# Key and value sums of two tiles: three more sums in one PSUM accumulator, with ScalarE copies between, and 44 weighings on VectorE

## The chip, the cores and the metric

One core of a Trainium2 chip runs the whole kernel. The time is device microseconds of one execution; the number compared is the median of several runs. The engines are TensorE (PE, with its weight loads as PEld), VectorE (DVE), ScalarE (ACT), GpSimd (POOL) and SyncE (SP, which here only issues transfers). Each works through its own queue in order, and they meet through semaphores.

## The reference

A graph attention layer with a residual and a layer norm, all in 32-bit floats: 16 graphs ("batches") of 1024 nodes with 512 features, 8 heads of 64, and one sparse adjacency matrix shared by all batches. The biases are zero in the inputs.

```python
q = (x @ Wq + bq).reshape(b, n, H, HD)
k = (x @ Wk + bk).reshape(b, n, H, HD)
v = (x @ Wv + bv).reshape(b, n, H, HD)
scores = jnp.einsum('bqhd,bkhd->bhqk', q, k) / jnp.sqrt(jnp.float32(HD))
scores = scores + (1.0 - adj)[None, None, :, :] * -1000000000.0
attn = jax.nn.softmax(scores, axis=-1)
out = jnp.einsum('bhqk,bkhd->bqhd', attn, v).reshape(b, n, d)
y = out @ Wo + bo
return layernorm(x + y)          # over the features
```

## The kernel before

The kernel uses that the adjacency matrix has few ones. It sorts the nodes by degree, cuts them into eight tiles of 128, and then works on "blocks": a block is 128 queries with one key each. For a block, GpSimd gathers 128 rows of keys and values (tile kvg) from DRAM; VectorE multiplies query and key (qk, L1313) and sums over each head (s, L1317); ScalarE takes the exponential (L1328); the value row is then weighed with it. The weighing has two forms in `weigh`: eight ScalarE instructions, one for each head (L1341), or one VectorE instruction (L1345). `by_act` says which block takes which. VectorE adds the weighed values up (L1357), or, for the nodes of high degree, TensorE does with a 0/1 matrix (L1366, L1367). A finished tile is normalised, transposed (poT, oT), multiplied by Wo (po, L799), and ends in the residual, the norm and a scatter to the output.

Ahead of that, for each batch, x is gathered, transposed on TensorE (pxT, xT) and multiplied by the weights. Tiles go in pairs, four pairs (j = 0 to 3) to a batch. `pair` makes the list of TensorE units of one pair. The queries are plain products (pq: `q0` for the first tile of the pair, `q1` for the second; each is four units of the function `product`). Tile 1, whose nodes have a single key each, has no queries after batch 0, so in the first pair of a batch `q1` is empty; and in the batches from 2 on tile 0 has queries only in every second batch, so there `q0` can be empty too.

Keys and values of a pair are made with seven half-size products instead of eight, by a scheme of the Strassen-Winograd kind. The weights are combined once into T1 to T4, beside the quarters B11, B21 and B22. For each pair VectorE forms four combinations s1 to s4 of the transposed inputs (`combine`, L783 to L786). A unit is two matmuls of 128x512 in the source, four in the profile (32-bit operands pass in two). Before the change, the units write to an accumulator x (twice), an accumulator z (twice), and to three banks p6, p7, p4 taken from four shared "fill" banks, which also serve all other products. The sums between them are made outside TensorE:

- ScalarE copies x to e after the first unit (L969), and x to the key of tile 0 after the second (L835);
- VectorE makes w = p6 + e (L972), g = p7 + w (L975), the key of tile 1 as p4 + g (L979), the value of tile 1 as z + g (L984) after z's first unit, and the value of tile 0 as z + w (L988) after its second.

The very first pair of all is computed plainly; 63 pairs use the scheme.

The order of all instructions is written out by hand in a loop of steps, one for each block (the `while` loop near the end). A step issues the block work first, then the functions that were planned for it with `later` (copies out of PSUM among them), then TensorE units out of the list `fronts` (or those of a finished tile, `finishing`, which go first) as long as a credit lasts. A step's credit is a share of the batch's remaining work, weighted by `load_of`. A unit has a cost, a function and a condition. If the unit at the head of the list is not ready, nothing more of the list is issued in that step. A unit that needs a copy made earlier (x's and z's second) is ready once that copy has been issued to its engine.

Of the kernel before, what the change touches and what calls it, by code (L numbers as in the profile page):

```python
# [71 lines left out]
LAST_SHARE = 3.4  # L72
BIAS = 0.22

P = 128
# [103 lines left out]
def kernel(  # L179
# [75 lines left out]
    with ExitStack() as main:  # L255
# [480 lines left out]

        BOTH = {}
        X, XT, SX, KV, VSUM, NRM, Y, OT, PS = {}, {}, {}, {}, {}, {}, {}, {}, {}
        set_up = {}
# [12 lines left out]
        def transpose_x(b, t):  # L752
            def pe():
# [25 lines left out]

                def combine():  # L780
                    s = [work.tile([P, HD2], F32, tag=f"s{i}", name=f"s{i}_{b}_{t}", bufs=1 + i // 4) for i in (1, 2, 3, 4)]
                    x0, x1 = XT[b, t - 1], XT[b, t]
                    nc.vector.tensor_tensor(s[0], x1[:, 0:HD2], x1[:, HD2:D], op=OP.add)  # L783
                    nc.vector.tensor_tensor(s[2], x0[:, 0:HD2], x1[:, 0:HD2], op=OP.subtract)
                    nc.vector.tensor_tensor(s[1], s[0], x0[:, 0:HD2], op=OP.subtract)
                    nc.vector.tensor_tensor(s[3], x0[:, HD2:D], s[1], op=OP.subtract)  # L786
                    SX[b, t // 2] = s
# [4 lines left out]

        def product(name, lhs, w, out):

# [8 lines left out]

            return [(PRODUCT, lambda c=c: unit(c), None) for c in range(NPAIR)]

# [10 lines left out]
        def pair(b, j):  # L816
# [62 lines left out]
            def lone_product():  # L879
# [24 lines left out]

                return [(4 * BIAS, pe, None)]

            def lhs(i):
                return lambda c: XT[b, tt[i]][:, ts(c, P)]

            q0, q1 = (  # L910
                product(f"pq_{b}_{tt[i]}", lhs(i), W["q"], lambda p, i=i: out_q(i, p)) if b == 0 or tt[i] != ONE_KEY else []
                for i in range(2)
            )
            if j == 0 and b >= PAIRED_FROM:
                q0 = []
                if merged(b):
                    q0 = product(f"pq_{b}_0", lambda c: BOTH[b // 2][:, 1, c, :], W["q"], lambda p: out_q(0, p))
                    q0 += lone_product()
# [28 lines left out]

            def unit(bank, left, right, first, after, need):
                def pe():
                    if first:  # L950
                        R[bank] = fill_psum(f"p{bank}_{b}_{j}") if bank[0] == "p" else psum.tile(
                            [P, HALF], F32, tag=bank, name=f"{bank}_{b}_{j}", bufs=1
                        )
                    l = left()
                    for c in range(2):
                        nc.tensor.matmul(  # L956
# [4 lines left out]

                return [(2 * PRODUCT, pe, lambda: (need is None or need in R) and (b, j) in SX and bool(combined))]

            def temp(name):
                R[name] = work.tile([P, D], F32, tag=name, name=f"{name}_{b}_{j}", bufs=1)
                return R[name]

            def out_e():
                nc.scalar.copy(temp("e"), R["x"])  # L969

            def out_w():
                nc.vector.tensor_tensor(temp("w"), R["p6"], R["e"], op=OP.add)  # L972

            def out_g():
                nc.vector.tensor_tensor(temp("g"), R["p7"], R["w"], op=OP.add)  # L975

            def out_k1():
                kv = KV[b, tt[1]]
                nc.vector.tensor_tensor(kv[:, 0:D], R["p4"], R["g"], op=OP.add)  # L979
                send(1)  # L980
                later_last(1, lambda: norm(b, tt[1], kv[:, 0:D]))

            def out_v1():
                nc.vector.tensor_tensor(new_kv(1)[:, D:], R["z"], R["g"], op=OP.add)  # L984
                R["v1"] = True

            def out_v0():
                nc.vector.tensor_tensor(KV[b, tt[0]][:, D:], R["z"], R["w"], op=OP.add)  # L988
                send(0)

            def s(i):
                return lambda: SX[b, j][i - 1]

            units = []
            units += unit("x", lambda: a(0, 0), B11, True, out_e, None)
# [334 lines left out]
        def by_act(n):  # L1330
# [168 lines left out]
        def paced(share, n):  # L1499
# [16 lines left out]
        with tc.manual_schedule():  # L1516
# [21 lines left out]
            while n < total or plan or rest or urgent or done or finishing or spilled or lone_tiles or not guarded:  # L1538
# [53 lines left out]
                while credit > 0 or urgent:  # L1592
# [10 lines left out]
                    if not units:  # L1603
# [54 lines left out]
```

## Time and profile before

| | |
|---|---|
| median of 3 runs | 1856.82 us (1855.36 to 1866.84) |
| span of the profiled execution | 1840.4 us |
| own time of the profiled execution | only its span is given; the median of the runs is 16.4 us above it |
| PE busy | 1798.2 us, 98%, 5140 matmuls |
| VectorE busy | 1693.7 us, 92% |
| ScalarE busy | 1563.2 us, 85% |
| GpSimd busy | 1215.3 us, 66% |
| granted TensorE clock | 0.996 on average |

A row of the groups names line, engine, operation, the tiles written and read, the shape and the count; after the first bar the busy time in us and the mean ns of one, after the second the idle time just before and what ended it. A row of the waits reads "engine line <- what released it: total us, times, longest us". A row of the timeline reads start in us, length in us, engine and instruction; in brackets the idle time before it and what released it. Matmuls overlap one another, so their pace is read from start to start.

### The profile page before, as it was taken

The page shows a single profiled execution, that of the slowest core. Times are in us where ns is not written, and L with a number is a line of the kernel's source. Part 1 is how long each engine was busy: PE and PEld are TensorE (multiplying, and loading weights), DVE is VectorE, ACT ScalarE, POOL GpSimd, SP SyncE. Part 2 cuts the span into 40 slices and gives each one's busy share as a digit, 9 for nine tenths or more (in the row PEclk, how much of TensorE's full clock was granted, in tenths as well). Part 3 has the DMA queues.
Part 4 walks back from the last instruction along what each step waited for, and adds up shares of the span by engine and source line. Part 5 has one row for each costly group of instructions (what it writes and reads, how often), then busy time and mean ns, then how long its engine had stood idle before and what let it go on. Part 6 is the DMA issues. An engine that isn't in the chain of part 4 may idle for free.

```text
span 1840.4 us, 25352 instructions
## 1 busy us (share of the span) xinstructions
PE 1798.2 (98%) x5140; PEld 876.2 (48%) x5140; DVE 1693.7 (92%) x3473; ACT 1563.2 (85%) x6183; POOL 1215.3 (66%) x1142
## 2 busy tenths in 40 slices
PE   7999999999999999999999999999999999999997
PEld 3444454554444454444444445444544444444443
DVE  6889889999989999999999999999999999997986
ACT  3637869989889898999889988989799999987886
POOL 1367766766565776767757666677666767665786
PEclk9999999999999999999999999999999999999998
DMA  7358787989889899999988998999989999889995
GB/s 287 106 190 253 256 325 237 346 301 327 308 280 314 295 336 319 344 316 308 347 316 310 346 335 276 343 321 322 339 315 325 314 355 326 306 324 325 338 319 191
DMA packets 198791, 558.54 MB, mean 303 GB/s; under 512 B 33450, under 2 KB 33470, under 8 KB 198626
## 3 DMA queue, kind: packets, MB, share of 16 engines
q0 software_dynamic: 112640, 370.50, 59.3%
q1 hardware_dynamic: 82910, 180.52, 26.2%
q10 hardware_dynamic: 3076, 5.82, 0.9%
q14 instruction: 122, 1.00, 0.2%
q8 instruction: 43, 0.70, 0.2%
HBM read 420.30 MB, written 157.45 MB: 314 GB/s over the span
## 4 chain that ended last, share of the span: by engine, by line
PE 69%; DVE 10%; ACT 9%; DMA 4%; issue 3%; POOL 1%; SPq 0%; POOLq 0%; DVEq 0%; ACTq 0%
PE po L799 17%; PE pq L799 15%; PE pp L956 12%; PE z L956 9%; PE x L956 9%; ACT pv L1341 5%; DVE qk L1313 2%; PE poT L1401 2%; PE pxT L757 2%; PE sum L1367 2%; DVE s L1317 2%; PE sum L1366 2%; DVE pv L1357 1%; ACT sq_k L809 1%; DMA kvg<-kv_pair,place_row 1%
## 5 line engine op out<-in xcount | busy, mean ns | idle before, releaser
L1341 ACT ACTIVATE pv<-kvg,pv 128x64 f32<-128x64 f32 x3600 | 907.5, 341 | 0.0
L1292 POOL DMA_INDIRECT kvg<-kv_pair,place_row x462 | 526.7, 1140 | 307.4 <-ACT pv L1341 99.6
L799 PE MATMUL pq<-wq,xT 128*128 128x512 f32 x792 | 367.8, 596 | 0.0
L1317 DVE TENSOR_REDUCE s<-qk 128x8 f32<-128x512 f32 x530 | 360.7, 681 | 6.8
L799 PE MATMUL po<-wo,oT 128*128 128x512 f32 x792 | 359.3, 594 | 0.7 <-ACT oT L1405 0.7
L1313 DVE TENSOR_TENSOR qk<-qt,kvg 128x512 f32<-128x512 f32 x434 | 297.2, 685 | 1.1 <-DMA kvg<-kv_rows,key_row 0.6
L956 PE MATMUL x<-b,xT 128*128 128x512 f32 x504 | 237.3, 593 | 0.5 <-ACT e L969 0.4
L956 PE MATMUL pp<-t,s 128*128 128x512 f32 x504 | 237.0, 593 | 0.0
L1357 DVE TENSOR_TENSOR pv<-pv,pv 128x520 f32<-128x520 f32 x329 | 228.3, 694 | 4.3 <-ACT pv L1341 4.2
L799 PEld LDWEIGHTS po<-wo,oT 128*128 128x128 f32 x792 | 149.1, 191 | 170.0 <-issue 160.2
L799 PEld LDWEIGHTS pq<-wq,xT 128*128 128x128 f32 x792 | 148.4, 192 | 161.9 <-issue 149.9
L1010 POOL DMA_INDIRECT x<-in_x_dram,asked_row x120 | 133.0, 1108 | 77.8 <-issue 21.3
L1148 POOL DMA_INDIRECT out_dram<-y,asked_row x129 | 146.9, 1139 | 39.1 <-issue 21.2
L1328 ACT ACTIVATE pv<-s,absent 128x8 f32<-128x8 f32 x434 | 127.0, 294 | 44.0 <-DVE s L1317 40.8
L809 ACT ACTIVATE sq_k<-kv 128x128 bf16<-128x128 f32 x512 | 150.8, 301 | 6.4 <-DVE kv L979 3.4
L956 PEld LDWEIGHTS pp<-t,s 128*128 128x128 f32 x504 | 94.7, 191 | 108.1 <-issue 99.4
L956 PEld LDWEIGHTS x<-b,xT 128*128 128x128 f32 x504 | 94.2, 191 | 107.4 <-issue 99.0
L956 PE MATMUL z<-b,s 128*128 128x512 f32 x252 | 119.2, 596 | 7.0 <-DVE kv L984 7.0
L1246 POOL DMA_INDIRECT qg<-q_rows,query_row x96 | 104.4, 1088 | 28.4 <-issue 26.9
L956 PE MATMUL z<-t,s 128*128 128x512 f32 x252 | 118.6, 593 | 0.0
L956 PE MATMUL pp<-t,xT 128*128 128x512 f32 x252 | 118.5, 593 | 0.0
L1134 ACT ACTIVATE y<-y,stats 128x512 f32<-128x512 f32 (+1 forms) x128 | 102.7, 806 | 17.0 <-DVE stats L1129 17.0
(279 smaller groups left out, 2713.0 us busy)
## 6 DMA issues: line engine op xcount, KB each, us to landing
kv_pair<-kv SPq DMA_DIRECT2D x98, 512.0 KB
q_rows<-q SPq DMA_DIRECT2D x106, 256.0 KB
qt<-q_rows SPq DMA_DIRECT2D x98, 256.0 KB
residual<-x SPq DMA_DIRECT2D x83, 256.0 KB
y<-residual SPq DMA_DIRECT2D x83, 256.0 KB
kv_rows<-kv SPq DMA_DIRECT2D x15, 512.0 KB
kvg<-kv_pair,place_row POOLq DMA_INDIRECT x462, 6.9
kv_pair<-kv SPq DMA_DIRECT2D x28, 256.0 KB
```

What stands on the lines that cost most here:

```text
L799: nc.tensor.matmul(p, lhs(c), w[:, c, :], start=(c == 0), stop=(c == NPAIR - 1))
L809: nc.scalar.activation(sq, s[:, ts(h, P)], AF.Square, scale=scale, accum_out=sums[:, h:h + 1])
L956: nc.tensor.matmul(R[bank], l[:, ts(c, P)], right[:, c, :], start=(first and c == 0), stop=(c == 1), skip_group_check=True,)
L1010: nc.gpsimd.indirect_dma_start(out=y, out_offset=None, in_=x_rows, in_offset=bass.IndirectOffsetOnAxis(ap=asked_row[:, t:t + 1], axis=0), ...
L1148: nc.gpsimd.indirect_dma_start(out=out_rows[b, t], out_offset=bass.IndirectOffsetOnAxis(ap=rows, axis=0), in_=y, in_offset=None, element_o ...
L1246: nc.gpsimd.indirect_dma_start(out=q, out_offset=None, in_=q_rows[b % ROWS], in_offset=bass.IndirectOffsetOnAxis(ap=rows, axis=0))
L1292: nc.gpsimd.indirect_dma_start(out=KG[n], out_offset=None, in_=rows, in_offset=bass.IndirectOffsetOnAxis(ap=(place_row if b else key_row)[ ...
L1313: nc.vector.tensor_tensor(QK[n], q, KG[n][:, 0:D], op=OP.mult)
L1317: nc.vector.tensor_reduce(S[n], QK.pop(n).rearrange("p (h d) -> p h d", d=HD), axis=AX.X, op=OP.add)
L1328: nc.scalar.activation(PV[n][:, D:], S.pop(n), AF.Exp, bias=bias)
L1341: nc.scalar.activation(pv[:, ts(h, HD)], v[:, ds(D + h * HD, HD)], AF.Copy, scale=pv[:, D + h:D + h + 1])
L1357: nc.vector.tensor_tensor(PV[b, t], PV[b, t], pv, op=OP.add)
```

## The change

In the 48 pairs with j > 0, x takes four units in a row: B11, then T2 with s2, T3 with s3, and T4 with the second tile's half, each added to what x already holds. After each of the four ScalarE copies x out: to the key half of tile 0 (what was e), to the value half of tile 0 (what was w), to the value half of tile 1 (what was g) and to the key half of tile 1, which is then complete. VectorE adds p2 (B21's product) to the key half of tile 0, and z to the value halves. In the first pair of a batch the five VectorE additions stay, with e, w and g held in the key and value tiles; the units are put in another order (p7 and the transposes before x's second unit, p4 before z's first), and the value of tile 1, which overwrites g, is issued only after its key, which reads g.

`busy` keeps a unit that opens x or z from being issued before the last copy out of it was, and keeps `combine` from being issued before the units that read the old s1 to s3 were. `next_unit` looks through the first ten units of the list for one that is ready, instead of at the head alone, but never past a transposition. And `by_act` gives ScalarE two in five of the blocks to which it gave one in two: 44 weighings go to VectorE.

```diff
@@ START
+LOOK = 10
@@ combine
+                    if busy["s"]:
+                        later(1, combine)
+                        return
+                    busy["s"] = 3
@@ pair / unit
+                def ready():
+                    if (b, j) not in SX or not combined or need is not None and need not in R:
+                        return False
+                    return not first or not busy.get(bank)
+
                 def pe():
                     if first:
+                        busy[bank] = bank in ("x", "z")
...
                     l = left()
+                    if any(l is t for t in SX[b, j][:3]):
+                        busy["s"] -= 1
@@ pair, after unit
+            def copied(name, i, v, bank="x"):
+                def fn():
+                    if (b, tt[i]) not in KV:
+                        new_kv(i)
+                    nc.scalar.copy(half_of(i, v), R[bank])
+                    R[name] = True
+
+                return fn
+
+            def added(i, v, bank):
+                nc.vector.tensor_tensor(half_of(i, v), R[bank], half_of(i, v), op=OP.add)
...
+            if j:
...
+                units += unit("x", lambda: a(0, 0), B11, True, copied("e", 0, False), None)
+                units += q0[:3]
+                units += unit("x", s(2), T2, False, copied("w", 0, True), "e")
+                units += q0[3:]
+                units += xt
+                units += unit("z", s(1), T1, True, out_v1, None)
+                units += unit("x", s(3), T3, False, copied("g", 1, True), "w")
+                units += q1
+                units += unit("x", lambda: a(1, 1), T4, False, out_k1, "g")
+                units += unit("p2", lambda: a(0, 1), B21, True, out_k0, None)
+                units += unit("z", s(4), B22, False, out_v0, "v1")
+                return units
...
+            units += unit("x", lambda: a(0, 0), B11, True, copied("e", 0, False), None)
             units += unit("p6", s(2), T2, True, out_w, None)
             units += q0
-            units += unit("x", lambda: a(0, 1), B21, False, lambda: out_k(0, R["x"]), "e")
             units += unit("p7", s(3), T3, True, out_g, None)
             units += xt
-            units += unit("z", s(1), T1, True, out_v1, None)
+            units += unit("x", lambda: a(0, 1), B21, False, out_k0, "e")
+            units += unit("p4", lambda: a(1, 1), T4, True, out_k1_added, None)
+            units += unit("z", s(1), T1, True, out_v1_last, None)
             units += q1
-            units += unit("p4", lambda: a(1, 1), T4, True, out_k1, None)
             units += unit("z", s(4), B22, False, out_v0, "v1")
@@ by_act
-            return n < total - NBT and (turn_of % 2 == 0 or n < NBT // 2)
+            return n < total - NBT and (turn_of % 5 in (1, 3) or n < NBT // 2)
@@ the loop of steps
+        def next_unit(units):
+
+            for i, (cost, _, ready) in enumerate(units[:LOOK]):
+                if cost == TRANSPOSE and i:
+                    return None
+                if not ready or ready():
+                    return i
+            return None
...
-                    cost, fn, ready = units[0]
-                    if ready and not ready():
+                    at = next_unit(units)
+                    if at is None:
...
-                    del units[0]
+                    cost, fn, _ = units.pop(at)
```

More of the change, by code (lines that the diff above doesn't have):

```diff
@@ L791, in transpose_x, with product @@
             return [(TRANSPOSE, pe, lambda: (b, t) in X)]
-        def product(name, lhs, w, out):
+        def product(name, lhs, w, out, ready=None):
             def unit(c):
@@ L802, in unit @@
                     later(1, lambda: out(p))
-            return [(PRODUCT, lambda c=c: unit(c), None) for c in range(NPAIR)]
+            return [(PRODUCT, lambda c=c: unit(c), ready) for c in range(NPAIR)]
         def squares(name, s, sums, scale=1.0):
@@ L960, in pe @@
                     later(1, after)
[L962 to L975, printed above, removed]
@@ L985, in out_v1, with s @@
+            def added(i, v, bank):
+                nc.vector.tensor_tensor(half_of(i, v), R[bank], half_of(i, v), op=OP.add)
+            def s(i):
+                return lambda: SX[b, j][i - 1]
+            def out_v1():
+                if "g" not in R:
+                    later(1, out_v1)
+                    return
+                added(1, True, "z")
+                landed(1)
                 R["v1"] = True
             def out_v0():
-                nc.vector.tensor_tensor(KV[b, tt[0]][:, D:], R["z"], R["w"], op=OP.add)
@@ L989, in out_v0, with out_k1, out_k0 @@
[L989 to L995 removed]
+                added(0, True, "z")
+                landed(0)
+                busy["z"] = False
+            def out_k1():
+                copied("k1", 1, False)()
+                key_done(1)
+                busy["x"] = False
+            units = []
+            if j:
+                def out_k0():
+                    added(0, False, "p2")
+                    key_done(0)
+                units += unit("x", lambda: a(0, 0), B11, True, copied("e", 0, False), None)
[10 more added lines that the diff above has]
+                return units
```

44 lines of the change are left out of this document (35 added, 9 removed).

## The prediction

> **What bounds the kernel now.** I read the page first (busy shares and slices), then busy time by stretch, the groups by line, the waits of TensorE, ScalarE and VectorE, and last the timeline around the longest stall.
>
> ```profile
> span 1840.4 us, 25352 instructions
> PE 1798.2 (98%) x5140; PEld 876.2 (48%) x5140; DVE 1693.7 (92%) x3473; ACT 1563.2 (85%) x6183; POOL 1215.3 (66%) x1142
> ```
>
> Now three stretches; the columns are length, then busy time (instructions) of PE, PEld, DVE, ACT and POOL, then the granted clock, the DMA share and GB/s.
>
> ```profile
> 0.00:46.00 46.00, 36.58 (x87) 16.73 (x88) 28.55 (x32) 17.36 (x42) 7.66 (x28) 0.96 0.78 287
> 46.00:1794.00 1748.00, 1728.90 (x4975) 844.75 (x4974) 1634.74 (x3350) 1514.70 (x6055) 1179.63 (x1085) 1.00 0.88 307
> 1794.00:1840.00 46.00, 32.66 (x82) 14.67 (x80) 30.39 (x93) 31.13 (x88) 28.03 (x29) 0.88 0.53 194
> ```
>
> Between 46 and 1794 us TensorE is idle for 1748.00 - 1728.90 = 19.1 us in all. The 9.4 us idle in the first 46 us and the 13.3 us in the last 46 us belong to loading and to the end of the last batch, which the change hardly touches. Whether a busy TensorE is really at its pace is seen in the timeline, from start to start:
>
> ```profile
> 911.68 1.88 PE L956 MATMUL x<-b,xT 128*128 128x512 f32 x4
> 913.40 1.88 PE L956 MATMUL pp<-t,s 128*128 128x512 f32 x4
> 915.12 3.60 PE L799 MATMUL po<-wo,oT 128*128 128x512 f32 x8
> 918.55 0.60 PE L1401 MATMUL poT<-ident,o 128*128 128x128 f32 x4
> ```
>
> A unit of four 128x512 matmuls takes 913.40 - 911.68 = 1.72 us, and eight take 918.55 - 915.12 = 3.43 us: 0.43 us each without a gap, across accumulators and lines. So TensorE is the bound, VectorE is second, and both other engines wait for TensorE more often than it waits for them:
>
> ```profile
> PE z L956 <- DVE kv L984: 7.0, 5, 3.0
> PE poT L1401 <- DVE stats L1123: 3.1, 1, 3.1
> PE x L956 <- ACT e L969: 0.4, 1, 0.4
> ACT e L969 <- PE x L956: 83.4, 36, 8.5
> DVE kv L984 <- PE z L956: 13.1, 13, 2.2
> ```
>
> The columns are total us, times and longest. The first row is the stall that the change works on: 7.0 of the 19.1 us.
>
> **What the change does to engine time.** No matmul goes or comes. A pair of tiles had seven units (x twice, p6, p7, p4, z twice) and has seven after it (x four times, z twice, p2). That row of TensorE's sum is nothing, so 19.1 us is the most that can be won between 46 and 1794 us.
>
> ```profile
> L1341 ACT ACTIVATE pv<-kvg,pv 128x64 f32<-128x64 f32 x3600 | 907.5, 341 | 0.0
> L1345 DVE TENSOR_TENSOR pv<-kvg,pv 128x512 f32<-128x512 f32 x80 | 54.9, 686 | 0.0
> L975 DVE TENSOR_TENSOR g<-pp,w 128x512 f32<-128x512 f32 x63 | 43.1, 684 | 13.6 <-PE pp L956 13.5
> L972 DVE TENSOR_TENSOR w<-pp,e 128x512 f32<-128x512 f32 x63 | 43.0, 683 | 3.1 <-PE pp L956 1.6 <-ACT e L969 1.4
> L969 ACT COPY e<-x 128x512 f32<-128x512 f32 x63 | 36.5, 580 | 83.4 <-PE x L956 83.4
> ```
>
> There are 63 pairs on the fast scheme (the first is computed plainly); 15 of them open a batch (j = 0) and 48 do not. In the 48, VectorE's five additions become three and ScalarE's two copies become four: VectorE loses 48 x 2 x 0.684 = 65.7 us, ScalarE gains 48 x 2 x 0.580 = 55.7 us. A weighing is eight ScalarE instructions, 907.5 / 450 = 2.02 us, or one VectorE instruction of 0.686 us: 44 of them take 88.7 us off ScalarE and put 30.2 us on VectorE. Net: VectorE -35.5 us (2.1% of 1693.7), ScalarE -33.0 us (2.1% of 1563.2). Both engines lie beside a full TensorE, so this is worth nothing by itself; it only shortens the stalls in which TensorE waits for them. Of the 19.1 - 7.0 = 12.1 us that are not the z stall I give 4 us to it (one third; bounds 0 and 12.1).
>
> A weighing on VectorE comes one step later than on ScalarE, so 44 kvg buffers come free later.
>
> ```profile
> POOL kvg L1292 <- ACT pv L1341: 110.4, 85, 6.2
> DVE qk L1313 <- DMA kvg<-kv_pair,place_row: 1.3, 2, 0.8
> ```
>
> GpSimd's gathers already wait 110.4 us for such buffers, and VectorE feels 1.3 us of it, so I cost the lateness at nothing; the gathers issued eight steps ahead are what hides it, and were they no longer enough, a few 0.8 us waits would show. SyncE's transfers and GpSimd's gathers are as many as before; a key/value buffer is held from the pair's first copy on, but of five only two belong to a pair, so I cost that at nothing too. The two PSUM uses that leave the four shared banks can only free TensorE.
>
> **The z bank, pairs with j > 0.** z's second unit waits until VectorE has added its first out. Between the two stood q1 and p4 (3.43 + 1.72 = 5.15 us); now x, q1, x and p2 stand there (8.6 us). The one stall of this kind was 1.06 us, and it goes: -1 us.
>
> **The z bank, the 15 pairs that open a batch.** There q1 is empty (tile 1 has no queries of its own after batch 0), so only p4 stood between, 1.72 us, and that is where the rest of the 7.0 us is, the longest three in these rows:
>
> ```profile
> 549.82 1.98 PE L956 MATMUL z<-b,s 128*128 128x512 f32 x4 [2.38 <-DVE kv L984]
> 1065.88 1.98 PE L956 MATMUL z<-b,s 128*128 128x512 f32 x4 [3.01 <-DVE kv L984]
> 1480.54 1.98 PE L956 MATMUL z<-b,s 128*128 128x512 f32 x4 [0.39 <-DVE kv L984]
> ```
>
> That is 7.0 - 1.06 = 5.9 us in 15 pairs. The changed order puts p4 ahead of z's first unit, so nothing of this pair stands between any more, and the hand-over gets longer. z's first unit is the last reader of s1 to s3, so the guard lets the next pair's four combinations out in the very next step, ahead of the k1 and v1 additions in VectorE's queue. Around the first of these stalls the trace shows what these cost:
>
> ```profile
> 542.96 1.88 PE L956 MATMUL z<-t,s 128*128 128x512 f32 x4
> 544.95 0.43 DVE L783 TENSOR_TENSOR s<-xT 128x256 f32<-128x256 f32 x1 [2.96 <-PE z L956]
> 546.08 0.42 DVE L786 TENSOR_TENSOR s<-xT,s 128x256 f32<-128x256 f32 x1
> 546.42 0.69 DVE L1112 TENSOR_TENSOR y<-po,y 128x512 f32<-128x512 f32 x1
> 549.08 0.68 DVE L984 TENSOR_TENSOR kv<-z,g 128x512 f32<-128x512 f32 x1
> 549.68 0.68 DVE L979 TENSOR_TENSOR kv<-pp,g 128x512 f32<-128x512 f32 x1
> ```
>
> z ends at 542.96 + 1.88 = 544.84, the combinations start 0.11 us later and take 546.42 - 544.95 = 1.47 us to the next start, k1 takes 549.68 - 549.08 = 0.60 us to the next start, v1 0.68 us, and z follows 0.06 us after v1 (549.82 - 549.76): 2.9 us. Against it stands what the new look-ahead can bring in: up to four q products of the next pair (3.43 us, which would hide all), an output product of a finished tile, block sums. Bounds for 15 pairs: 0 us and 15 x 2.9 = 43.5 us. The nearest measured cover is p4's 1.72 us, and I take it that what the look-ahead and the other work bring is worth as much: 2.9 - 1.72 = 1.2 us each, 18 us, in place of 5.9: +12 us.
>
> **The x bank.** In 48 pairs x is now reused three times behind a ScalarE copy (144 hand-overs, where it was one per pair behind e). Between stand three q products (2.57 us), then one q product, two transposes and z (0.43 x 2 + 0.43 x 2 + 1.72 = 3.4 us), then q1 (3.43 us). A copy can start late, because ScalarE's queue is in order:
>
> ```profile
> 915.55 0.57 ACT L969 COPY e<-x 128x512 f32<-128x512 f32 x1
> ```
>
> Here x ended at 913.56, so the copy came 1.99 us late and was done 2.56 us after x: 2.57 us just hides it. In 36 of 63 cases ScalarE sat waiting for x (the row above) and the copy is done within 0.6 us or so. Waiting behind such a copy on ScalarE are weighings and exponentials, but they have their steps of slack. Bounds: 144 times the j > 0 rate of z with 5.15 us of cover (1.06 / 48 = 0.022 us, 3 us) and 144 times the j = 0 rate with 1.72 us of cover (5.9 / 15 = 0.39 us, 57 us). The copies are shorter than VectorE's queue there, so I stay near the low end: 0.03 us each, +4 us (rounded).
>
> **Sum.** -4 - 1 + 12 + 4 = +11 us; after rounding I forecast a profiled span of 1851 us. Around the span lie 1856.82 - 1840.4 = 16.4 us that the change leaves alone, so 1867 us. (The page's runs spread from 1855.36 to 1866.84; 1%, or 18.6 us, is about what a measurement here can tell from no change.) The case's own range, with z hand-overs from 0.4 to 1.6 us each and x from 0 to 0.08: -5 to +18 us.
>
> **The rivals.**
>
> *Stalls vanish.* The look-ahead covers every z hand-over with q products, ScalarE keeps up with x, and relief takes a third to all of the other 12.1 us. Then -6 to -19 us, typically 1846 us, and at the very most 1856.82 - 19.1 = 1837.7. For it: four of the five z stalls sit where the next pair's q products could have been. Against it: VectorE stays at 1658 of 1840 us.
>
> *The z hand-over lies bare, slower.* In the 15 opening pairs z's second unit follows at once in the next step, with a combination, k1 and v1 ahead of it on VectorE. It decides from about 1.7 us per pair on (15 x 1.7 - 5.9 = +20 us). With the whole 2.9 us and x at 0.08 us: 43.5 - 5.9 + 11.5 = +49 us, 1906; half way, with the other terms, about 1882 us. For it: the order as written leaves no unit of its own between, and a unit ends its step's budget often. Against it: only up to 1.3 us of cover is needed to stay under 1.7.
>
> *The clock drops.* One bank that is refilled behind copies makes TensorE stop more often, and a long stop costs more than itself:
>
> ```profile
> 1808.33 1.02 PE L1401 MATMUL poT<-ident,o 128*128 128x128 f32 x4 [3.09 <-DVE stats L1123]
> 1809.14 3.25 PE L799 MATMUL po<-wo,oTs 128*128 128x512 f32 x4
> ```
>
> After a stop of 3.09 us four matmuls took 3.25 us where 1.88 is usual: 1.4 us more. Once in each of 48 pairs that is +67 us, 1924 us. Against it: the granted clock is 1.00 over the whole middle stretch, with the 3.01 us stall in it. [...]
>
> *TensorE is not the bound.* If VectorE set the pace, its 35.5 us would come off: 1821 us. For it: VectorE is 94% busy in the middle stretch (1634.74 of 1748). Against it: the gapless 0.43 us. [...]
>
> **How the numbers follow.** The forecast case has 0.52, vanishing stalls 0.18, the bare z hand-over 0.26, the clock 0.02, VectorE as bound 0.02. Faster by over 1% (under 1838.2): the 0.02 of the last and 0.04 of vanishing stalls, with the spread of the runs: 0.06. Slower by over 1% (over 1875.4): the 0.02 of the clock, 0.24 of the bare hand-over and 0.02 of the forecast's upper end: 0.28. Within: 0.66. For 8 in 10 the range reaches from 1843 (most of the vanishing stalls) to 1888 (past the middle of the bare hand-over).
>
> **What would show it.** TensorE's 5140 matmuls and their busy time stay within a few us; VectorE's busy time falls to about 1658 and ScalarE's to about 1530 us; "PE z <- DVE" lies in opening pairs alone, with 18 us; "PE x <- ACT" rows for the four copies add to a few us. I am wrong if the z row shrinks below 5 us, if x's rows exceed 15 us, or if TensorE's idle time in the middle stays near 19 us while the span moves.

## The result: 3.9% slower, above the forecast range

The changed kernel took 1933.45 us (median of 4 runs, 1932.00 to 1938.52), the kernel before it 1861.83 us on the same chip: a ratio of 1.0388 (95% interval 1.0344 to 1.0432). The forecast was 1867 us, and its range ended at 1888. On a second chip both were timed again: 1910.30 against 1846.54 us, 1.0343 (1.0325 to 1.0362). The 1.0343 has the narrower interval, and below every kernel is compared by its ratio to the kernel before on its own chip.

The page of the changed kernel, its head and engine totals:

```profile
span 1932.7 us, 25008 instructions
PE 1826.6 (95%) x5140; PEld 881.5 (46%) x5140; DVE 1667.8 (86%) x3421; ACT 1532.5 (79%) x5927; POOL 1226.0 (63%) x1142
```

The matmuls are as many as before, VectorE lost 25.9 us and ScalarE 30.7 us, and the span is still 92 us longer. Some 20 us of that come from the profiled execution of before, which was quicker than the median of its runs, 1861.83 us. The stretches of the first chip's execution (length, then busy time and instructions of PE, PEld, DVE, ACT and POOL, then granted clock, DMA share, GB/s):

```profile
0.00:46.00 46.00, 34.55 (x80) 15.73 (x81) 28.73 (x33) 17.45 (x42) 7.67 (x28) 0.96 0.76 284
46.00:1886.00 1840.00, 1766.45 (x4998) 853.87 (x4996) 1612.71 (x3306) 1488.45 (x5813) 1195.10 (x1089) 0.99 0.85 293
1886.00:1933.00 47.00, 25.59 (x64) 11.88 (x63) 26.34 (x85) 26.59 (x73) 23.21 (x25) 0.80 0.39 138
```

In the middle TensorE is idle for 1840.00 - 1766.45 = 73.6 us (19.1 before), and the same matmuls are busy for longer. The second execution's waits of TensorE (total us, times, longest):

```profile
PE z L970 <- DVE kv L1001: 34.6, 14, 3.9
PE poT L1474 <- DVE stats L1196: 9.0, 1, 9.0
PE x L970 <- ACT kv L995: 4.6, 3, 2.4
```

z waits five times as long as before (7.0 us), and x's four copies cost next to nothing directly. In the first execution z's wait stands in two rows, and there is a single stop of 11.8 us that ends at 146 us (the row of pxT):

```profile
PE z L970 <- DVE kv L1001: 31.9, 12, 3.8
PE pxT L759 <- ACT xT L763: 11.8, 1, 11.8
PE z L970 <- issue: 5.7, 2, 3.6
```

One opening pair of the changed kernel in the timeline, VectorE and TensorE (start us, length us; in brackets the idle time before):

```profile
1333.03 1.88 PE L970 MATMUL z<-t,s 128*128 128x512 f32 x4
...
1334.95 0.43 DVE L789 TENSOR_TENSOR s<-xT 128x256 f32<-128x256 f32 x1 [2.34 <-issue]
1335.29 0.42 DVE L790 TENSOR_TENSOR s<-xT,xT 128x256 f32<-128x256 f32 x1
1335.63 0.42 DVE L791 TENSOR_TENSOR s<-s,xT 128x256 f32<-128x256 f32 x1
1336.08 0.42 DVE L792 TENSOR_TENSOR s<-xT,s 128x256 f32<-128x256 f32 x1
1336.42 0.68 DVE L1185 TENSOR_TENSOR y<-po,y 128x512 f32<-128x512 f32 x1
1337.14 0.69 DVE L1186 SCALAR_TENSOR_TENSOR y<-bo_bc,y 128x512 f32<-128x512 f32 x1
...
1337.76 0.69 DVE L1001 TENSOR_TENSOR kv<-z,kv 128x512 f32<-128x512 f32 x1
...
1338.50 3.78 PE L970 MATMUL z<-b,s 128*128 128x512 f32 x4 [3.59 <-DVE kv L1001]
...
1342.07 2.90 PE L970 MATMUL x<-b,xT 128*128 128x512 f32 x4
```

z's first unit ends at 1334.91; VectorE runs the next pair's four combinations and a finished tile's residual (two instructions, 0.68 and 0.69 us) before it adds z out at 1337.76. Nothing stands on TensorE for 3.59 us. Then comes the second thing to see: four matmuls that take 1.88 us elsewhere take 3.78 us. In that stretch the granted clock (the column after POOL) is half:

```profile
1338.50:1342.07 3.57, 3.57 (x4) 1.51 (x5) 1.75 (x3) 3.57 (x13) 2.19 (x2) 0.50 0.90 304
```

So the stop is paid a second time in clock.

### The profile page after: what moved, and what is told of

It is laid out like the page before. It is cut to its first block, busy times and chain, and to the rows that moved or that the text cites. A ratio compares the mean times of both kernels' runs of the same rounds, so it can differ in the third digit from the quotient of the medians.

```text
span 1932.7 us, 25008 instructions
## 1 busy us (share of the span) xinstructions
PE 1826.6 (95%) x5140; PEld 881.5 (46%) x5140; DVE 1667.8 (86%) x3421; ACT 1532.5 (79%) x5927; POOL 1226.0 (63%) x1142
## 5 line engine op out<-in xcount | busy, mean ns | idle before, releaser
L1414 ACT ACTIVATE pv<-kvg,pv 128x64 f32<-128x64 f32 x3248 | 818.8, 340 | 0.0
L1365 POOL DMA_INDIRECT kvg<-kv_pair,place_row x462 | 533.7, 1155 | 347.1 <-ACT pv L1414 90.0
L805 PE MATMUL pq<-wq,xT 128*128 128x512 f32 x792 | 374.2, 596 | 0.0
L995 ACT COPY kv<-x 128x512 f32<-128x512 f32 x222 | 129.0, 581 | 227.5 <-PE x L970 189.1
L970 PE MATMUL x<-t,s 128*128 128x512 f32 x384 | 181.1, 594 | 4.8 <-ACT kv L995 4.7
L970 PE MATMUL z<-b,s 128*128 128x512 f32 x252 | 132.2, 651 | 37.7 <-DVE kv L1001 31.9
L970 PE MATMUL x<-b,xT 128*128 128x512 f32 x312 | 152.5, 612 | 0.0
L1319 POOL DMA_INDIRECT qg<-q_rows,query_row x96 | 111.7, 1163 | 32.4 <-issue 27.0
L970 PEld LDWEIGHTS x<-t,s 128*128 128x128 f32 x384 | 72.0, 190 | 91.2 <-issue 79.2
L763 ACT COPY xT<-pxT 128x512 f32<-128x512 f32 x128 | 70.4, 577 | 41.8 <-PE pxT L759 19.5
```

The source lines that it names most:

```text
L805: nc.tensor.matmul(p, lhs(c), w[:, c, :], start=(c == 0), stop=(c == NPAIR - 1))
L970: nc.tensor.matmul(R[bank], l[:, ts(c, P)], right[:, c, :], start=(first and c == 0), stop=(c == 1), skip_group_check=True,)
L995: nc.scalar.copy(half_of(i, v), R[bank])
L1365: nc.gpsimd.indirect_dma_start(out=KG[n], out_offset=None, in_=rows, in_offset=bass.IndirectOffsetOnAxis(ap=(place_row if b else key_row)[ ...
L1414: nc.scalar.activation(pv[:, ts(h, HD)], v[:, ds(D + h * HD, HD)], AF.Copy, scale=pv[:, D + h:D + h + 1])
```

## Experiments

The theory at this point: the opening pairs' z hand-over lies bare (the second rival), and its long stops slow the clock besides (the third). Rival theories: the 48 other pairs' x chain costs it; the weighings cost it.

### Which part costs: undoing one part at a time

**open_old**: the opening pairs get their old order, additions and temporaries back; all else as changed.

```diff
-            units += unit("x", lambda: a(0, 0), B11, True, copied("e", 0, False), None)
+            units += unit("x", lambda: a(0, 0), B11, True, out_e, None)
             units += unit("p6", s(2), T2, True, out_w, None)
             units += q0
+            units += unit("x", lambda: a(0, 1), B21, False, out_k0, "e")
             units += unit("p7", s(3), T3, True, out_g, None)
             units += xt
-            units += unit("x", lambda: a(0, 1), B21, False, out_k0, "e")
-            units += unit("p4", lambda: a(1, 1), T4, True, out_k1_added, None)
-            units += unit("z", s(1), T1, True, out_v1_last, None)
+            units += unit("z", s(1), T1, True, out_v1_old, None)
             units += q1
-            units += unit("z", s(4), B22, False, out_v0, "v1")
+            units += unit("p4", lambda: a(1, 1), T4, True, out_k1_old, None)
+            units += unit("z", s(4), B22, False, out_v0_old, "v1")
```

> The 15 pairs that open a batch get the additions, the temporaries and the order of units of the kernel before (p4 between z's two units); everything else stays as changed. If the bare z hand-over in these pairs is the cause (33 us of waits in the profile of the changed kernel and some 17 us of half-speed matmuls behind them), the time falls by 40 to 55 us to 1880-1893, the 'PE z <- DVE' waits fall to 5-10 us and the granted clock goes back to 0.99 or more. If the x bank with its ScalarE copies is the cause, it stays above 1920. If the look-ahead's order of work is the cause, it stays above 1920 too and the z waits alone fall.

Measured: 1877.54 against 1848.41 us, 1.0151 (1.0131 to 1.0170). In the trace of this kernel z's waits have all but gone (the last two rows; L1065 is the addition in the opening pairs, L1001 that in the others), and other rows have not:

```profile
PE poT L1486 <- DVE o L1472: 9.5, 3, 9.0
PE pxT L759 <- DMA x<-in_x_dram,asked_row: 7.9, 4, 3.0
...
PE x L970 <- ACT kv L995: 7.1, 4, 3.1
...
PE z L970 <- DVE kv L1001: 2.9, 3, 1.4
...
PE z L970 <- DVE kv L1065: 1.8, 5, 0.6
```

So the opening pairs cost 1.0343 - 1.0151 = 0.0192, some 35 us, more than half of the loss. The rest is elsewhere.

**after_again**: the changed kernel once more, unedited, on another chip.

> The changed kernel itself, unedited, beside the next three on the same chip: 1.035 to 1.043 times the kernel before, z waits of 30 to 40 us and a granted clock of 0.98.

Measured 1.0343, as told above. The 11.8 us stop did not come back, so it is left out of what follows. Its cause was not found. Stops of this kind stand in the traces of weigh_only (11.4 us, ending at 143 us), pairs_old (6.7 us, ending at 137 us), open_old_weigh_old (10.0 us, at 167 us) and open_old_head (8.5 us, at 160 us), all below and all from one further chip. On that chip the kernel before ran at 1867.14 us, and no trace tells whether it stops there too; so these four ratios are less certain than their intervals say.

**pairs_old**: all 63 pairs on the old scheme; the look-ahead, the guards and the 44 weighings stay. **weigh_only**: the kernel before with the 44 weighings alone. **guards_only**: the kernel before with the look-ahead and the guards alone.

```diff
@@ weigh_only, against the kernel before
-            return n < total - NBT and (turn_of % 2 == 0 or n < NBT // 2)
+            return n < total - NBT and (turn_of % 5 in (1, 3) or n < NBT // 2)
@@ guards_only, against the kernel before
+LOOK = 10
...
+                    if busy["s"]:
+                        later(1, combine)
+                        return
...
+                    return not first or not busy.get(bank)
...
+                    cost, fn, _ = units.pop(at)
```

> All 63 pairs get the additions and the order of units of the kernel before; the look-ahead of ten units, the guards and the 44 weighings on VectorE stay. With the opening pairs alone restored the ratio to the kernel before was 1.015, some 28 us. If x's three hand-overs behind ScalarE are what is left, this falls to 1.000-1.004 (within 8 us of the kernel before). If the look-ahead, the guards or the weighings are what is left, it stays at 1.010-1.015.

> The kernel before with the changed choice of weighings alone: 44 of them on VectorE, so VectorE +30 us and ScalarE -89 us. If VectorE's load (92% before) is a bound beside TensorE, this costs 10 us or more. If only TensorE's waits count, it stays within 5 us. If the weighings are the gain in the change, it is 5 us or more faster.

> All pairs in the order and with the additions of the kernel before, and its weighings: only the look-ahead of ten and the guards are left of the change. The restored pairs with the new weighings gave 1.0025 and the new weighings alone 1.0052, so the look-ahead and the guards should give 0.997 to 0.998, 4 us faster than the kernel before. If they cost by themselves, it is above 1.000.

| kernel | us | before, same chip | ratio (95%) |
|---|---|---|---|
| pairs_old | 1870.96 | 1867.14 | 1.0025 (0.9989 to 1.0060) |
| weigh_only | 1875.36 | 1867.14 | 1.0052 (1.0024 to 1.0081) |
| guards_only | 1844.29 | 1846.54 | 0.9985 (0.9976 to 0.9994) |

The look-ahead and the guards are worth 0.15%. The weighings alone cost 0.5% (0.2 to 0.8%); the difference of pairs_old and guards_only, 0.4%, points the same way, but crosses chips, and pairs_old's own interval includes 1. Why they should cost anything on the old pairs no run shows. The x chain in the 48 pairs costs 1.0151 - 1.0025 = 0.0126, some 23 us. So guards_only, pairs_old, open_old and the whole change are four rungs of one ladder: -0.0015, +0.0040, +0.0126 and +0.0192 to 1.0343. (The rungs come from different chips, and pairs_old's interval alone is 0.007 wide, so some tenths of a per cent in the middle two are open, and the stops told of above lie in the second.)

### Why the opening pairs cost what they do

**combine_last**: the changed kernel with the next pair's combinations issued behind the step's planned additions. **cover_x**: the changed kernel with x's B21 unit moved between z's two units. **both**: both edits.

```diff
@@ combine_last
-                        later(1, combine)
+                        later_last(1, combine)
@@ cover_x
-            units += unit("x", lambda: a(0, 1), B21, False, out_k0, "e")
             units += unit("p4", lambda: a(1, 1), T4, True, out_k1_added, None)
             units += unit("z", s(1), T1, True, out_v1_last, None)
+            units += unit("x", lambda: a(0, 1), B21, False, out_k0, "e")
```

> The next pair's four combinations are issued after the planned additions of a step instead of ahead of them, nothing else changes. If they stand in VectorE's queue ahead of v1, v1 starts 1.47 us earlier after z's end in the opening pairs: z waits fall from 38 to some 18 us, most stops of TensorE fall under 2 us and the clock drops behind them go, so -30 us, about 1903. If VectorE's other work is what makes v1 late, the waits and the time stay within 5 us.

> In the opening pairs x's second unit moves from ahead of p4 to between z's two units: 1.72 us more of cover, the same work. If the hand-over is bare, z waits fall from 38 to 14 us, the clock drops with them, -35 us, about 1898. If x's copies or the rest is the cause, within 5 us of 1933.

> Both edits at once: v1 1.47 us earlier and 1.72 us of cover. By the hand-over theory the z waits all but vanish (under 5 us), clock 0.99 or more, about 1885 (-48 us), and what is left over the kernel before, some 20 us, is x's hand-overs and the start. By the x theory, within 5 us of 1933.

Measured: combine_last 1883.99 us, 1.0192 (1.0175 to 1.0209); cover_x 1885.57 us, 1.0201 (1.0182 to 1.0220); both 1879.70 us, 1.0168 (1.0151 to 1.0185), all against 1848.41 us. Against the changed kernel's 1.0343 that is 28, 26 and 32 us, where 30, 35 and 48 were expected from the first chip's time. The two don't add: both is level with open_old. The z rows of combine_last, cover_x and both, in this order:

```profile
PE z L970 <- DVE kv L1001: 15.9, 11, 2.6
```

```profile
PE z L970 <- DVE kv L1001: 12.2, 10, 2.4
```

```profile
PE z L970 <- DVE kv L1001: 3.4, 3, 2.6
```

Four combinations out of the way (1.47 us) or one unit of four matmuls as cover (1.72 us), and 34.6 us of waiting becomes 15.9 or 12.2. That is the mechanism of the second rival, both halves of it. The time won is not smaller than the rows, as it would be if other work waited next, but larger: from the changed kernel to combine_last the z row falls by 18.7 us and the time by 28 us; to cover_x by 22.4 us and 26 us.

**warm** and **warm2**: is the surplus the clock? Both add two matmuls of the source behind z's first unit in each opening pair, which write to a bank that nobody reads. They cannot make VectorE's addition come sooner; they only keep TensorE from standing still. In warm they read z's own operands, in warm2 constant weights; the lines are those of warm2, and warm differs in the two operands alone.

```diff
                     later(1, after)
+                    if j == 0 and bank == "z" and first:
+                        warm = fill_psum(f"warm_{b}")
+                        for c in range(2):
+                            nc.tensor.matmul(warm, B21[:, c, 0:P], B11[:, c, :], start=(c == 0), stop=(c == 1))
```

> The changed kernel with two more 512-column matmuls (1.72 us) behind z's first unit in the 15 opening pairs, into a bank that nobody reads; the result and every wait of v1 stay. If the long stops of TensorE cost a slower clock besides themselves, TensorE now stops for under 2 us there, the half-speed matmuls go (17 us of them in the changed kernel, 27 with the tail), and in the three pairs that had cover the dummies cost 5 us: the time falls by 10 to 15 us although work is added. If the clock has nothing to do with the stops, it stays or rises by up to 5 us.

> As the run with dummy matmuls, but the dummies read weights alone. In that run they read s1, so that the combinations, and v1 behind them, waited for the dummies too (v1 3.3 us after z instead of 2.2 in half of the pairs); half-speed matmuls fell by 11 us all the same. Now v1 should come as early as in the changed kernel. If a slower clock after the long stops costs time of its own, 11 us or so fall off 1.034 less 5 us of dummies that stand in the way: 1.029-1.032. If it does not, 1.034-1.037.

warm: 1916.13 us, 1.0381 (1.0360 to 1.0401), a miss, and confounded. Its extra matmuls read s1, so the next pair's combinations had to wait for them, and v1 behind those: in the pair of the timeline above v1 starts 4.56 us after z's end, where it was 2.85. warm2 has no such tie: 1898.40 us, 1.0270 (1.0254 to 1.0286). With 60 more matmul records it is 0.0073 (13 us) faster than the changed kernel, and the mean granted clock is 0.993 instead of 0.985. The pair of the timeline above, in warm2:

```profile
1301.04 1.88 PE L970 MATMUL z<-t,s 128*128 128x512 f32 x4
1302.76 1.88 PE L978 MATMUL warm<-b,b 128*128 128x512 f32 x4
...
1305.76 0.69 DVE L1005 TENSOR_TENSOR kv<-z,kv 128x512 f32<-128x512 f32 x1
1306.50 1.98 PE L970 MATMUL z<-b,s 128*128 128x512 f32 x4 [1.87 <-DVE kv L1005]
```

From z's end to v1 it is 1305.76 - 1302.92 = 2.84 us, as in the changed kernel (2.85), and z's second unit then takes 1.98 us instead of 3.78. The hand-over is unchanged; the slow matmuls behind it are gone. That the clock after a stop costs time of its own is thus shown; 13 of the 35 us are what it comes to here, give or take a few since the two kernels ran on different chips, and perhaps a little more, since the added matmuls could only cost.

### Where the 48 pairs' cost lies

**open_old_weigh_old**: open_old with the old share of weighings on ScalarE. **open_old_weigh_less**: with one block in five there instead of two. **open_old_head**: open_old without the look-ahead. **x_cover**: open_old with p2 and all of q0 used as cover between x's units. **copies_first**: open_old with x's copies at the head of their step, ahead of ScalarE's exponentials.

```diff
@@ open_old_weigh_old, open_old_weigh_less
-            return n < total - NBT and (turn_of % 5 in (1, 3) or n < NBT // 2)
+            return n < total - NBT and (turn_of % 2 == 0 or n < NBT // 2)
+            return n < total - NBT and (turn_of % 5 == 1 or n < NBT // 2)
@@ open_old_head
-LOOK = 10
+LOOK = 1
@@ x_cover
-                units += q0[:3]
+                units += q0
                 units += unit("x", s(2), T2, False, copied("w", 0, True), "e")
-                units += q0[3:]
+                units += unit("p2", lambda: a(0, 1), B21, True, out_k0, None)
...
-                units += unit("p2", lambda: a(0, 1), B21, True, out_k0, None)
@@ copies_first
-                    later(1, after)
+                    (later_first if j and bank == "x" else later)(1, after)
...
+                for fn in early.pop(n, ()):
+                    fn()
```

> Opening pairs as before, and the weighings as before too (ScalarE 89 us busier, VectorE 30 us less busy than in the run that restored the opening pairs alone). If x's copies on ScalarE come late because ScalarE is behind, x's hand-overs get worse: 5 to 15 us over that run's 1.015. If VectorE at the end of the program (a 9 us wait of the last transposition for VectorE) is what is left, it falls by 5 to 10 us.

> Opening pairs as before the change, and ScalarE weighs one in five of the blocks that it weighed one in two of, instead of two in five: ScalarE some 80 to 90 us less busy than at 1.015, VectorE 30 us more. If ScalarE's lateness at x's copies and at the copies that free the shared banks is what the 48 pairs cost, it falls to 1.005-1.010. If VectorE is as near to its limit, it stays or rises to 1.02.

> Opening pairs as before, and the look-ahead cut to the head of the list (as in the kernel before); x's four units, the guards and the weighings stay. If the look-ahead is what lets other work cover x's copies, units stop a step earlier and the time rises by 10 us or more over 1.015. If the look-ahead's order is what costs the remaining 28 us, it falls to about 1.00.

> Opening pairs as before the change; in the other 48 pairs the same units in another order: the fourth q product ahead of x's second unit and p2 between x's second and third, so 3.43, 4.3 and 3.43 us of cover instead of 2.57, 3.45 and 3.43, and 1.72 instead of 3.44 before the next pair's x. If x's hand-overs are what costs 24 us in these pairs, 5 to 12 us fall off the 1.015 of that order (to about 1.009-1.012). If the cost is the length of the chain in steps, it stays within 5 us.

> Opening pairs as before the change; the four copies out of x are issued at the head of their step on ScalarE, ahead of the exponential that waits for VectorE's sums, instead of behind it. If the order of ScalarE's queue makes them late, x's waits fall from 7 us to under 3 and the time by 3 to 8 us (1.011-1.013). If ScalarE's load makes them late, within 3 us of 1.015.

| kernel | us | before, same chip | ratio (95%) | TensorE's x row |
|---|---|---|---|---|
| open_old | 1877.54 | 1848.41 | 1.0151 (1.0131 to 1.0170) | 7.1 us, 4 times |
| open_old_weigh_old | 1906.46 | 1867.14 | 1.0208 (1.0167 to 1.0248) | 27.9 us, 11 times |
| open_old_weigh_less | 1867.96 | 1848.37 | 1.0104 (1.0088 to 1.0119) | 7.2 us, 4 times |
| open_old_head | 1901.57 | 1867.14 | 1.0201 (1.0164 to 1.0238) | 14.1 us, 4 times |
| x_cover | 1873.00 | 1846.54 | 1.0138 (1.0120 to 1.0157) | 7.2 us, 6 times |
| copies_first | 1866.56 | 1848.37 | 1.0098 (1.0082 to 1.0113) | 6.2 us, 4 times |

More cover between x's units left x's row as it was: 7.2 us in x_cover, 7.1 in open_old. x_cover's time, within the intervals of open_old, does not settle it, for p2 was taken from ahead of z's second unit, and z's row grew from 2.9 us:

```profile
PE z L970 <- DVE kv L1001: 10.9, 6, 4.4
```

Without the look-ahead (open_old_head) the time is 0.005 longer; 8.5 of its 14.1 us in the x row are the one stop named above. How far ScalarE is behind seems to be part of it, but not through x's own row. With the old weighings the x row is 27.9 us, 17.9 without the stop of 10.0, and the kernel slower by 0.0057; so 44 weighings that seem to cost 0.5% on the old pairs seem to earn about 0.6% beside the chain, as far as ratios from two chips can tell. With still fewer (weigh_less), and with the copies first, the time falls by 0.005 each while the x row stays at 6 to 7 us. In copies_first some 6 of the 10 us were gained at the end of the kernel, on the last tiles' way to the output: the long wait of a transposition, 9.0 us in open_old above, is

```profile
PE poT L1491 <- DVE stats L1213: 3.1, 1, 3.1
```

as long as in the kernel before. But weigh_less has the same time and keeps that wait (9.0 us), so it gained elsewhere.

**chain_mended**: open_old with copies_first (x's copies in the opening pairs too), combine_last and one weighing in five, all three together.

> The change with all that the runs so far point to: opening pairs as before, copies out of x at the head of the step, combinations behind the planned additions, one in five weighings on ScalarE instead of two in five. Apart, the last three gave -5, -5 and, in the changed kernel, -30 us of which the opening pairs took most. If the costs are ScalarE's lateness alone, they add up: 1.003 to 1.007, still not faster than the kernel before, since TensorE's 19 us of idle time there were all that was to be won. If VectorE's load takes over, 1.010.

1861.39 against 1849.02 us, 1.0071 (1.0054 to 1.0088). The rows of TensorE that are clearly longer than before's:

```profile
PE pxT L764 <- DMA x<-in_x_dram,asked_row: 8.4, 2, 5.3
PE x L975 <- ACT kv L1000: 7.0, 5, 2.6
```

Before, the first was 0.4 us and x's row 0.4 us: together 14.6 us more, near the 12 to 13 us by which this kernel is slower than before. Both stand in open_old too (7.1 and 7.9 us). The x row is the chain's own. Beside pairs_old, open_old tells the same: x's copies 7.1 us, where pairs_old has no such row; the late gather 7.9 us, where pairs_old has none; and 9.5 us before transpositions of a finished tile, where pairs_old has 3.6:

```profile
PE poT L1468 <- DVE o L1454: 3.6, 2, 2.8
```

These three come to some 21 of the chain's 23 us. Why the gather of x's rows for a transposition comes late beside the chain was not found, and no run here separates it, so it is only argued that the chain causes the late gather.

### A version that is faster than both

**guards_last**: guards_only with the combinations issued behind the planned additions (the edit of combine_last). **guards_last_first**: that, with x's copies first.

> The kernel before with the look-ahead and the guards (0.9985), and the combinations issued behind the planned additions. If VectorE's order costs z's hand-overs in that kernel too (7 us of excess), 3 to 5 us: 0.996. If not, 0.998-1.000.

> The kernel before with the look-ahead, the guards and the combinations behind the additions (0.9948), and its two copies out of x at the head of the step. These copies are covered by 5.15 us and cost 0.4 us of waits in the kernel before, so within 3 us: 0.993 to 0.997.

guards_last: 1839.19 against 1848.37 us, 0.9948 (0.9934 to 0.9961). It keeps the old pairs and the old weighings and takes the look-ahead, and the z row falls to 1.3 us, from 7.0 in the kernel before and 5.1 in guards_only:

```profile
PE z L970 <- DVE kv L1047: 1.3, 3, 1.0
```

guards_last_first: 1844.64 against 1849.02 us, 0.9980 (0.9969 to 0.9991). Putting the copies first gained beside the chain and loses without it; a miss, whose cause is open. So of the whole change its smallest part, with the combinations issued later in their step, was worth 9 us against the kernel before. (The two ratios 0.9985 and 0.9948 come from different chips.) What made the change slow is the new pairs, and perhaps the weighings.

## Why the prediction was wrong, step by step

**The bound: right.** TensorE sets the time; matmuls stayed at 5140. VectorE's load fell to 1667.8 us (1658 forecast) and ScalarE's to 1532.5 (1530), and the time rose all the same, so "VectorE as bound" fell. TensorE's busy time did not stay within a few us, as the prediction had it: it rose from 1798.2 to 1826.6 us, with the same matmuls at a lower clock (0.980 on average, 0.996 before).

**Relief of 4 us: not seen.** No run has the relief of both engines by itself. The weighings alone, one half of it, made the kernel slower by 0.5% (0.2 to 0.8%); beside the chain they seem to help. The prediction counted the relief as engine time and costed a weighing that comes a step later at nothing; whether that step is what costs was not tested.

**Cover for z's hand-over in the opening pairs: the step that failed most.** The prediction gave this term +12 us; putting the opening pairs back (open_old) won some 35 us. The prediction costed the bare hand-over at 2.9 us and took off 1.7: p4's cover, and the belief that what the look-ahead brings is worth as much. The 2.9 us were a little low (from z's end to its second unit it is 2.3 to 4.4 us in twelve opening pairs, 3.5 on average, for other additions stand in VectorE's queue besides; the rows it showed had this too, 549.82 - 544.84 = 4.98 us with a finished tile's addition and v1 ahead). But the look-ahead brought a full cover in three pairs alone (a finished tile's output product); in the other twelve nothing stood there, or two to four matmul records (of q products, block sums, bias products, transpositions), and TensorE was idle for 1.3 to 3.8 us. In these twelve pairs that comes to 33.3 us in the first execution and 33.7 in the second, instead of 18; the bare bound was 43.5. The second rival had the place and the mechanism, with a chance of 0.26, but its dearest case, 1906 us, still lay 27 us under the result: the clock and the cost of the other 48 pairs were not in it. The argument held against it, that "only up to 1.3 us of cover is needed", stood on no row. p4 had been taken out from between; its worth could not be kept in the sum on the strength of a look-ahead that no trace showed. (The sum's own upper end was added up wrongly besides: -4 - 1 + 18 + 11.5 is +25 us, not +18. It would not have reached the result either.)

**The clock as a rival of its own, at 0.02: wrong.** It is no alternative to the bare hand-over but its second half: a longer stop may be paid again in slow matmuls, as the stop of 3.59 us above was (3.78 us instead of 1.88). The prediction had even shown the case (3.25 us instead of 1.88 after 3.09 us) and set it aside because of the clock of 1.00 in the middle of the kernel before. Behind the stop of 3.59 us one matmul takes 0.85 us instead of 0.43, and the mean clock is 0.985 in the second execution instead of 0.996 before; the size of it is the 13 us of warm2, not the rival's 67.

**x's hand-overs at 4 us: right for the row, wrong for the chain.** The row was 4.6 us in the second execution, 7.1 in open_old. But the 48 pairs cost some 23 us. What the runs show is that some 6 us of it lay at the end of the kernel (one transposition that waited 9.0 us instead of 3.1), that a late gather of x is another 8 us, and that the cost falls as ScalarE has less to do. What ties the gather and ScalarE's load to the chain stays open. The prediction had looked for the cost only where the new waits are; of what queues behind a late copy on ScalarE it said that "they have their steps of slack", and the sensitivity to ScalarE's load speaks against that.

**16.4 us around the span: wrong, and without effect.** The profiled execution of the changed kernel took 1934.45 us with a span of 1932.7: 1.75 us lie around it. The profiled execution of before was simply quicker than the three runs beside it. The forecast's +11 us, 0.6%, does not hang on it.

Of what was to show it: x's row stayed under 15 us, as foreseen; the z row lay almost wholly in the opening pairs, as foreseen, with nearly twice the time; TensorE's idle time in the middle rose from 19.1 to 73.6 us together with the span, and its busy time rose too, which was not foreseen.

## What to carry to other kernels

When a change takes work from between two uses of one PSUM bank, price the hand-over bare, and take off only cover that a row of the trace shows in that place; what a freer order may bring in is a rival, not a term of the sum. A stop of TensorE can have two prices, the wait and slow matmuls after it (here they followed stops of 2.17 and 3.59 us, and did not follow others of 2.78 and 3.58), so they belong in one case. And when an edit is a bundle, its smallest part may be what pays: here the look-ahead, with the combinations moved behind the additions that release a bank.

## What the runs showed of the hardware that was not expected

Whether a stop was followed by slow matmuls was not decided by its length alone. TensorE's second units of z in three opening pairs of the changed kernel's first execution (in brackets the stop before them):

```profile
587.57 1.98 PE L970 MATMUL z<-b,s 128*128 128x512 f32 x4 [2.78 <-DVE kv L1001]
...
906.57 3.20 PE L970 MATMUL z<-b,s 128*128 128x512 f32 x4 [2.17 <-DVE kv L1001]
...
1338.50 3.78 PE L970 MATMUL z<-b,s 128*128 128x512 f32 x4 [3.59 <-DVE kv L1001]
```

The third of these pairs in its second execution:

```profile
1318.17 1.98 PE L970 MATMUL z<-b,s 128*128 128x512 f32 x4 [3.58 <-DVE kv L1001]
```

After 3.59 us the four matmuls were slow, after 3.58 us in the other execution they were not; after 2.17 us they were slow, after 2.78 not. The granted clock was 0.50 in the four matmuls from 1338.50 on, as shown above, 0.61 in those from 906.57 on and 1.00 in those from 587.57 on. In the second execution it was 1.00 behind the 3.58 us:

```profile
1318.17:1322.00 3.83, 3.83 (x9) 1.82 (x10) 3.56 (x6) 3.75 (x14) 2.39 (x3) 1.00 0.95 312
```

The slow spell, where it is seen whole, covers seven matmuls from 1338.50 on, six of them at 0.85 us or more from start to start. What decides whether a stop is followed by such a spell was not shown.

The other thing: guards_only and guards_last differ by the place of four short instructions of each pair in VectorE's queue, and stand at 0.9985 and 0.9948, on different chips; 44 weighings, 30 us of work moved to VectorE, changed the old pairs by some 0.5%, little more than that.
